# Two Toeplitz layers of a four-layer network: coefficient tables in small pieces, an unpadded product tensor, and a projection in two passes by columns

## The chip, the cores and the metric

The kernel runs on one core of a Trainium2 chip. The metric is the device time of one execution in microseconds, given as the median of the runs. The profile is one more execution, recorded instruction by instruction.

## The reference

The input x has 8 samples of 56 x 56 positions with 192 channels, all in f32. Four layers follow each other, each of the form x + layer(group norm of x). Layers 0 and 1 are alike, and the change lies in them:

```python
p = silu(x @ p_w.T + p_b); q = silu(x @ q_w.T + q_b); v = silu(x @ v_w.T + v_b)   # 192 -> 576
a1 = rpe_mlp(lags, t1...) * decay; a2 = rpe_mlp(lags, t2...) * decay              # 111 lags x 576
qv = q * v
o1 = toeplitz(qv along w, a1); o2 = toeplitz(qv along h, a2)
out = (p * (o1 + o2)) @ o_w.T + o_b                                               # 576 -> 192
```

A Toeplitz product along one axis is, for each of the 576 channels, a 56 x 56 matrix whose entries depend on the lag alone, multiplied by the 56 values of a row or column. Layer 2 is a 7 x 7 depthwise convolution with an MLP, layer 3 a windowed attention.

## The kernel before

Samples are worked on in pairs: `j0 = 0` and `j0 = 2` each stand for two of the four pairs, that is for half of the batch. Each of the two layers has, for each half, three generators that emit instructions and yield their estimated time:

- Q(i, j0), `tno_qv` (L221): for tokens in groups of 256, it loads x (L237, on SP), normalizes it (L243, on ACT), multiplies it by the weights of q and v in units of 128 tokens and 512, 512 and 128 columns (L260, on PE), adds the bias (L269, on DVE), applies silu (L298, ACT), multiplies q by v (L301, POOL) and stores the product in DRAM (L304, SP), in the tensor `qv` of half j0. The loop over columns lies inside the loop over tokens. The first Q is special: its first two groups go through `half_unit` (L281), so that it can begin when the statistics of the first pair are there.
- TZ(i, j0), `tno_toeplitz` (L362): for 9 blocks of 64 channels, and for both axes d (so 18 rounds n), it loads `qv` into the tile `q` (L376 for d = 0, two strided loads; L379 for d = 1, one load of 128 rows, 64 for each half of the block, of which 56 hold data and 8 hold zeros) and the matrices `tm` (L389, four loads), multiplies (L402), copies the result out of the banks (L409, ACT), turns it (L420, L422, DVE), adds the second axis (L424, POOL) and stores the sum (L434, POOL's queue). The loads of round n + 2 are issued when round n has been emitted.
- O(i, j0), `tno_out` (L474): for tiles of 224 tokens, it loads x and the sums (L119, L499), makes p (L527 to L546), multiplies (L553) and projects (L562 to L588), stores the next x and takes its statistics.

A channel block of TZ needs `qv` of all tokens, for its own 64 channels. A pass of Q yields all channels at once.

`decay_tables` (L136) makes the Toeplitz coefficients of one layer: powers of the decay (L146 to L158, DVE), a small MLP (L179 on PE, L181 on DVE), and for each of two axes and five channel groups one matmul (L185), two operations on DVE (L192) into a tile `a` of which there are two, and up to four stores to DRAM (L202). It is a plain function: everything is emitted where it is called.

`tno_layers` (L666) sets the order. First comes a head, in which the statistics of the input (`input_stats`, L207) and the first Q are interleaved by hand, the tables of layer 0 and of layer 1 are called at two places, and rows of zeros are written to `qv` (L715). Then `weave` (L629) runs lanes: the generators of a lane one after the other, and beside them the steps of one TZ. It gives TZ its next step when

```python
want = (done / total - lo) / (hi - lo) * given     # lo 0.04, hi 0.92
while steps is not None and gave < want: ...
```

so that TZ advances in proportion to the lane's estimated time; whatever remains of TZ is emitted when the last generator of the lane has come to 0.9 of its time. From the first TZ on, PE, ACT, DVE and POOL run in the order in which instructions were emitted. The lanes before are:

```python
lanes = [[(first, QT - 104.0)], [(Q(0, 2), QT)], [(O(0, 0), OT), (Q(1, 0), QT)]]
lanes += [[(O(0, 2), OT), (Q(1, 2), QT)], [(O(1, 0), OT)], [(O(1, 2, False), OT)]]
```

with QT = 298.1 and OT = 299.6. Beside lanes 1 to 4 stand TZ(0,0), TZ(0,2), TZ(1,0) and TZ(1,2). Lane 5 runs beside the convolution of layer 2.

Of the kernel before, what the change touches and what calls it, by code (L numbers as in the profile page):

```python
# [12 lines left out]
F32 = mybir.dt.float32  # L13
# [13 lines left out]
B, H, W, C = 8, 56, 56, 192  # L27
T = H * W
# [15 lines left out]
class Net:  # L44
# [91 lines left out]
    def decay_tables(self, L, p, tables):  # L136

        nc, inp = self.nc, self.inp
        tv = p.tile([32, 111], F32, name="tv", bufs=1)
        nc.sync.dma_start(tv, inp["tvec"])  # L140
        pows = []
        for c in range(5):
            m = min(128, D1 - 128 * c)
            sl = p.tile([128, 1], F32, name="sl")
            nc.sync.dma_start(sl[:m], inp[f"{L}_slope"][128 * c : 128 * c + m, :])
            nc.vector.tensor_scalar(sl[:m], sl[:m], 0.0, 1.0, ALU.max, ALU.min)  # L146
            nc.vector.tensor_scalar(sl[:m], sl[:m], 1.0 - 0.95, 0.95, ALU.mult, ALU.add)
            pw = p.tile([128, 64], F32, name="pw", bufs=5)
            nc.gpsimd.memset(pw[:m, 0:1], 1.0)
            n = 1  # L150
            while n < 64:
                nc.vector.tensor_scalar(
                    pw[:m, n : 2 * n], pw[:m, 0:n], sl[:m], None, ALU.mult
                )
                n *= 2
                if n < 64:
                    sq = p.tile([128, 1], F32, name="sl")
                    nc.vector.tensor_mul(sq[:m], sl[:m], sl[:m])  # L158
                    sl = sq
            pows.append(pw)  # L160
        for d in range(2):
            t = f"{L}_t{d + 1}"
            w0 = p.tile([32, 2], F32, name="w0")
            nc.sync.dma_start(w0[:, 0:1], inp[f"{t}_w0"])
            nc.sync.dma_start(w0[:, 1:2], inp[f"{t}_b0"])
            ws = p.tile([32, 3, 32], F32, name="ws")
            nc.sync.dma_start(ws, inp[f"{t}_ws"])
            bs = p.tile([32, 3], F32, name="bs")
            nc.sync.dma_start(bs, inp[f"{t}_bs"])
            wo = p.tile([32, D1], F32, name="wo")  # L170
            nc.sync.dma_start(wo, inp[f"{t}_wo"])
            bo = p.tile([128, 5], F32, name="bo")
            nc.sync.dma_start(bo, inp[f"{t}_bo"])
            h = p.tile([32, 111], F32, name="h")
            nc.vector.tensor_scalar(h, tv, w0[:, 0:1], w0[:, 1:2], ALU.mult, ALU.add)
            nc.vector.tensor_scalar(h, h, 0.0, None, ALU.max)
            for i in range(3):
                hp = self.bank2()[:32, 0, :111]
                nc.tensor.matmul(hp, ws[:, i, :], h, start=True, stop=True)  # L179
                h = p.tile([32, 111], F32, name="h")  # L180
                nc.vector.tensor_scalar(h, hp, bs[:, i : i + 1], 0.0, ALU.add, ALU.max)  # L181
            for c in range(5):
                m = min(128, D1 - 128 * c)
                ap = self.bank2()[:, 0, :111]
                nc.tensor.matmul(  # L185
                    ap[:m], wo[:, 128 * c : 128 * c + m], h, start=True, stop=True
                )
                a = p.tile([128, 4 * self.TG + 56], F32, name="a")
                nc.gpsimd.memset(a[:m, 111:], 0.0)
                back = view(pows[c][:m], 55, [[-1, 55]])  # L190
                for lo, hi, dec in ((0, 55, back), (55, 111, pows[c][:m, 0:56])):
                    nc.vector.scalar_tensor_tensor(  # L192
                        view(a[:m], 110 - lo, [[-1, hi - lo]]),
                        ap[:m, lo:hi],
                        bo[:m, c : c + 1],
                        dec,
                        ALU.add,
                        ALU.mult,
                    )
                for n in range(m // 32):  # L200
                    to = tables[d][self.TG * (4 * c + n) : self.TG * (4 * c + n + 1)]
                    nc.sync.dma_start(  # L202
                        to.rearrange("g (c w) -> c g w", w=self.TW),
                        view(a[32 * n : 32 * n + 32], 0, [[4, self.TG], [1, self.TW]]),
                    )

    def input_stats(self, xs, gn, j, p):  # L207

# [9 lines left out]
        for more in self.all_norms():  # L218
            pass

    def tno_qv(self, L, j0, xs, gn, qv, apart=None):  # L221

# [117 lines left out]
        for g in range(2 if apart else 0, groups):  # L342
            x, t0, n = loaded.pop(0)
            for s in range(0, n, 128):
                m = min(128, n - s)
                for c0 in range(0, 2 * D1, 512):
                    k = min(512, 2 * D1 - c0)

                    if late is not None:
                        multiply(*late)  # L350
                    if c0 == 512 and s + 128 >= n and g + 1 < groups:
                        normalize(*loaded[0])
                    z = p.tile([128, 512, 4], F32, name="t8")
                    unit(x, s, m, c0, k, z)
                    late = (m, k, z, t0 + s, c0)
                    if c0 == 0 and s == 0 and g + 2 < groups:
                        loaded.append(load(g + 2))
                    yield 5.3 * k / 512
        multiply(*late)
# [2 lines left out]
    def tno_toeplitz(self, j0, mats, qv, o):  # L362
# [6 lines left out]
        def load(n):  # L369
            blk, d = divmod(n, 2)  # L370
            q = p.tile([128, H, 128], F32, name="q", bufs=2)
            if d == 0:

                for half in range(2):
                    of = qv[2 * blk + half, :T].rearrange("(h w) e -> w h e", w=W)
                    nc.sync.dma_start(q[64 * half : 64 * half + W], of)  # L376
            else:
                of = qv[2 * blk : 2 * blk + 2].rearrange("n (h w) e -> (n h) (w e)", w=W)
                nc.sync.dma_start(q.rearrange("p i e -> p (i e)"), of)  # L379
            return q  # L380

        def matrices(n):
# [283 lines left out]
    def tno_layers(self, x0, x1, x2, gn, last):  # L666
# [11 lines left out]
        ]  # L678
        qvs = {

            j0: self.dram.tile([D1 // 32, 64 * W, 128], F32, name=f"qv{j0}") for j0 in (0, 2)
        }
        o = [self.dram.tile([B // 2, 9, 128, T], F32, name=f"{L}_sum") for L in LS]
        x = (x0, x1, x2)
        with ExitStack() as ctx, ExitStack() as wqp:
            self.wqp = wqp.enter_context(tc.tile_pool(name="wqp", bufs=1, side="right"))
            self.tp = ctx.enter_context(tc.tile_pool(name="tp", bufs=3))
            Q = lambda i, j0, apart=None: self.tno_qv(LS[i], j0, x[i], gn[i], qvs[j0], apart)
            O = lambda i, j0, woven=True: self.tno_out(LS[i], j0, x[i], gn[i], o[i], x[i + 1], gn[i + 1], woven)
            TZ = lambda i, j0: self.tno_toeplitz(j0, tables[i], qvs[j0], o[i])  # L690
            QT, OT, TZT = 25 * 2.25 * 5.3, 28 * 10.7, 8 + 72 * 3.2
# [1 line left out]
            with tc.tile_pool(name="tab", bufs=2) as tab:  # L693
                stats = [self.input_stats(x0, gn[0], j, tab) for j in range(4)]
                for more in stats[0]:
                    pass
                first = Q(0, 0, tab)
                next(first)

                for n in range(14):  # L700
                    next(first)
                    next(stats[1], None)
                for more in stats[1]:
                    pass
                for n in range(10):
                    next(first)
                self.decay_tables("L0", tab, tables[0])
                for st in stats[2:]:
                    for more in st:
                        next(first)  # L710
                none = tab.tile([112, 512], F32, name="none", bufs=1)
                nc.gpsimd.memset(none, 0.0)
                for qv in qvs.values():
                    to = qv[:, T:].rearrange("n (p k) e -> p n (k e)", p=112)
                    nc.gpsimd.dma_start(to, view(none, 0, [[0, D1 // 32], [1, 512]]))  # L715
                self.decay_tables("L1", tab, tables[1])
                for t in tables:
                    for d in range(2):
                        nc.gpsimd.dma_start(t[d][D1 // 32 * self.TG :, :512], none[:1])
                lanes = [[(first, QT - 104.0)], [(Q(0, 2), QT)], [(O(0, 0), OT), (Q(1, 0), QT)]]  # L720
                lanes += [[(O(0, 2), OT), (Q(1, 2), QT)], [(O(1, 0), OT)], [(O(1, 2, False), OT)]]
                self.weave(lanes[0], None, lanes[1][0][0])
            in_order = tc.manual_schedule(engines=ENGINES)
            with tc.tile_pool(name="tz", bufs=1) as self.tz, in_order:
                self.tms = []
# [1 line left out]
                    self.tms.append(self.tz.tile([128, 32 * self.TW], F32, name=f"tm{i}"))  # L727
                for n, tz in enumerate((TZ(0, 0), TZ(0, 2), TZ(1, 0), TZ(1, 2))):
                    self.weave(lanes[n + 1], tz, lanes[n + 2][0][0], TZT)
                    if n == 2:  # L730
                        wqp.close()
            self.weave(lanes[5], **last())


# [906 lines left out]
```

## Time and profile before

| | us |
|---|---|
| median of three runs (lowest, highest) | 5861.83 (5849.73, 5865.73) |
| the profiled execution | 5859.99 |
| its span | 5858.2 |
| PE busy in it | 5356.5 (91%) |
| DVE, ACT, POOL busy | 2365.6, 2269.0, 2206.4 |
| mean granted clock of PE | 0.954 |

Of the groups of instructions, the costliest is L260 on PE with 1286.6 us; L402 has 525.6 us. In the tables by stretch below, each row is a stretch of the span in us from its start, then its length, and the time in it in which each engine was busy, with the number of instructions in brackets; then come the granted clock of PE (1.00 is full), the mean busy share of the 16 DMA engines (packets overlap, so that it may pass 1) and the rate in GB/s. A line of waits names who waited, for what, how many us in total, how often, and the longest.

### The profile page before, as it was taken

How to read it: one execution, taken by the hardware profiler on the slowest of the kernel's cores; microseconds unless marked ns; L12 is line 12 of the kernel's file. 1: busy time of each engine (PE TensorE's matmuls, PEld its weight loads, DVE VectorE, ACT ScalarE, POOL GpSimd, SP SyncE). 2: the span in 40 equal slices, each digit the busy share in tenths (PEclk: the TensorE clock that was granted, in tenths of full speed). 3: DMA queues.
4: the chain of work that ended last, by engine and by line, in shares of the span. 5: the costliest groups of instructions: out<-in, count | busy, mean ns of one | idle time of the engine just before them, and what ended most of it. 6: DMA issues, size and time to landing. Idle time of an engine off the chain costs nothing.

```text
span 5858.2 us, 144266 instructions
## 1 busy us (share of the span) xinstructions
PE 5356.5 (91%) x64672; PEld 3886.7 (66%) x64672; DVE 2365.6 (40%) x3770; ACT 2269.0 (39%) x2990; POOL 2206.4 (38%) x1527
## 2 busy tenths in 40 slices
PE   5799888899999999999888799989999999889887
PEld 2577666677777777777666578856665445667666
DVE  5444554233454233553343322331222322556655
ACT  2244454444454444554444322242323333333332
POOL 1244566466556564565666300000001001333332
PEclk8799999999999999999999899999999999999998
DMA  8547998898787887987999465644444222344442
GB/s 268 110 144 219 267 287 245 220 264 275 214 237 217 239 258 224 254 249 196 312 296 293 168 210 205 230 125 161 150 160 121 64 64 62 75 97 86 89 92 56
DMA packets 1029770, 1098.79 MB, mean 188 GB/s; under 512 B 232768, under 2 KB 966976, under 8 KB 1013728
## 3 DMA queue, kind: packets, MB, share of 16 engines
q1 hardware_dynamic: 993568, 888.57, 55.5%
q0 software_dynamic: 35584, 200.99, 8.9%
q8 instruction: 509, 8.34, 0.6%
q14 instruction: 109, 0.89, 0.0%
HBM read 725.48 MB, written 363.94 MB: 186 GB/s over the span
## 4 chain that ended last, share of the span: by engine, by line
PE 57%; POOL 6%; SPq 6%; DMA 5%; DVE 5%; issue 3%; ACT 2%; POOLq 0%; DVEq 0%; ACTq 0%
PE bank L260 9%; PE bank L950 6%; PE bank L811 5%; PE bank L527 4%; PE bank L1030 4%; PE bank L572 4%; PE bank L402 4%; SPq L389 3%; PE bank L1044 3%; POOL s L424 2%; PE bank L1224 2%; PE bank L536 2%; PE bank L575 2%; SPq L376 2%; PE bank L1171 2%
## 5 line engine op out<-in xcount | busy, mean ns | idle before, releaser
L260 PE MATMUL bank<-wq,t 128*128 128x256 f32 (+4 forms) x7680 | 1286.6, 375 | 66.8 <-DVE t L269 36.3
L260 PEld LDWEIGHTS bank<-wq,t 128*128 128x128 f32 (+2 forms) x7680 | 1006.5, 191 | 348.1 <-issue 110.5
L269 DVE TENSOR_TENSOR t<-bank,wq 128x1024 f32<-128x1024 f32 (+3 forms) x480 | 517.8, 1111 | 776.6 <-PE bank L260 575.1
L301 POOL TENSOR_TENSOR t<-t 128x1024 f32<-128x1024 f32 (+2 forms) x288 | 518.7, 1815 | 692.4 <-ACT t L298 371.5
L409 ACT COPY ot<-bank 128x896 f32<-128x896 f32 x576 | 493.2, 914 | 626.8 <-PE bank L402 351.3
L424 POOL TENSOR_TENSOR s<-s,ot 128x1568 f32<-128x1568 f32 x144 | 618.3, 4298 | 70.0 <-DVE ot L422 69.3
L402 PE MATMUL bank<-q,tm 56*32 56x224 f32 x18432 | 525.6, 365 | 81.6 <-DMA tm<-L_tab 26.8
L298 ACT ACTIVATE t<-t 128x2048 f32<-128x2048 f32 (+2 forms) x288 | 422.0, 1488 | 405.7 <-DVE t L269 396.1
L402 PEld LDWEIGHTS bank<-q,tm 56*32 56x32 f32 x18432 | 354.4, 109 | 221.6 <-issue 115.8
L553 POOL TENSOR_TENSOR t<-t,t 128x896 f32<-128x896 f32 x168 | 347.3, 2085 | 358.4 <-DMA t<-L_sum 163.9
L527 PE MATMUL bank<-t,wo 128*128 128x224 f32 x1792 | 398.0, 378 | 46.6 <-ACT t L506 22.1
L585 DVE SCALAR_TENSOR_TENSOR t<-bank,wo,t 128x448 f32<-128x448 f32 x112 | 76.4, 682 | 886.3 <-ACT t L581 474.7
L950 PE MATMUL bank<-z,w 128*128 128x448 f32 (+1 forms) x1344 | 413.7, 555 | 1.9 <-ACT h L959 1.7
L527 PEld LDWEIGHTS bank<-t,wo 128*128 128x128 f32 x1792 | 352.4, 203 | 83.8 <-issue 31.7
L546 ACT ACTIVATE t<-bank,wo 128x448 f32<-128x448 f32 x448 | 248.1, 635 | 407.2 <-PE bank L536 379.2
L572 PE MATMUL bank<-t,wo 128*128 128x224 f32 x1792 | 378.1, 365 | 0.0
L127 POOL DMA_DIRECT2D x<-x x64 | 36.6, 573 | 859.7 <-DVE x L981 829.6
L572 PEld LDWEIGHTS bank<-t,wo 128*128 128x128 f32 x1792 | 337.2, 194 | 33.8 <-issue 32.2
L811 PEld LDWEIGHTS bank<-xt,cm 113*112 113x112 f32 x3072 | 315.0, 180 | 43.7 <-issue 38.3
L420 DVE STREAM_TRANSPOSE s<-ot 128x1792 f32<-128x1792 f32 x144 | 292.5, 2033 | 124.3 <-DMA L_sum<-s 102.1
L811 PE MATMUL bank<-xt,cm 113*112 113x108 f32 (+2 forms) x3072 | 326.2, 266 | 6.4 <-issue 3.3
L950 PEld LDWEIGHTS bank<-z,w 128*128 128x128 f32 (+1 forms) x1344 | 182.2, 189 | 205.7 <-issue 197.4
(148 smaller groups left out, 6991.3 us busy)
## 6 DMA issues: line engine op xcount, KB each, us to landing
q<-qv SPq DMA_DIRECT2D x36, 3584.0 KB
q<-qv SPq DMA_DIRECT2D x72, 1568.0 KB
L_sum<-s POOLq DMA_DIRECT2D x288, 392.0 KB, 7.4
t<-L_sum SPq DMA_DIRECT2D x112, 1008.0 KB
qv<-t SPq DMA_DIRECT2D x192, 512.0 KB
cm<-in_L_cm SPq DMA_DIRECT2D x96, 896.0 KB
tm<-L_tab SPq DMA_DIRECT2D x288, 240.0 KB
x<-t POOLq DMA_DIRECT2D x112, 336.0 KB, 7.1
```

Of the source, the lines that this page charges most:

```text
L260: nc.tensor.matmul(pp[:m, b, 256 * j : 256 * j + k], x[rows, j, 2 if part else b, s : s + m], w[rows, part, c0 + c : c0 + c + k],  start=p ...
L269: nc.vector.tensor_add(z[:m, c : c + k, :], view(pp[:m], 0, [[1, k], [256, 4]]), view(bias[:m], c0 + c, [[1, k], [0, 4]]),)
L298: nc.scalar.activation(z[:m, :n, :], z[:m, :n, :], AF.Silu)
L301: nc.gpsimd.tensor_mul(prod[:m, :k], half[:, :, 0], half[:, :, 1])
L402: nc.tensor.matmul(pt[32 * j : 32 * j + 32, r, hf * 224 : (hf + 1) * 224], tm[rows, at : at + 32], q[rows, :, 4 * c : 4 * c + 4], start=Tr ...
L409: nc.scalar.copy(view(ot, 4 * (g % 4), [[16, 2], [32, 112], [1, 4]]), view(pt, 0, [[512, 2], [4, 112], [1, 4]]),)
L424: nc.gpsimd.tensor_add(to, to, view(of, 0, [[1, 28], [32, 56]]))
L527: mm(gs[c // 2][:, b, c % 2 * 256 : c % 2 * 256 + N], pw[:, 0, 128 * c : 128 * c + 128], xn[:, b], start=c % 2 == 0, stop=False,)
L553: gate.tensor_mul(to, to, pg)
L572: mm(P[:, b, :N], ow[:, c, 0:128], g[:, 4 * b + c], start=False, stop=c == 3 and b == 1)
L811: nc.tensor.matmul(pc[:, 128 * e + 4 * m0 : 128 * e + 4 * m1], cm[:113, e, k, :], xt[:, m0 - 1 + k : m1 - 1 + k, c + e, :], start=n == 0 a ...
L950: nc.tensor.matmul(phs[c][:, s, :TT], w0[rows, part, at : at + 128], z[rows, Z[2 if part else s], :], start=part == flip, stop=part != flip,)
```

## The change

- `decay_tables` becomes a generator with 21 yields for a layer. Both layers' tables are one stream `decay` of 42 pieces: 14 are taken beside the statistics of the third and fourth pair, one after each step of the first Q, and the remaining 28 beside the rest of the first Q, by `weave` with lo 0 and hi 0.75.
- `qv` has T = 3136 rows for each channel group instead of 64 x 56 = 3584; the writing of zeros goes, and the load for d = 1 becomes two loads of 56 rows. Rows 56 to 63 and 120 to 127 of the tile `q` are not loaded; no matmul reads them.
- `tno_qv` takes a range of columns. Q(1,2) becomes two generators: columns 0 to 511 (channel blocks 0 to 3) in lane 3, behind O(0,2), and columns 512 to 1151 (blocks 4 to 8) at the head of lane 4, ahead of O(1,0). Each of them loads and normalizes x. TZ(1,2) begins at the start of lane 4 as before, which is now behind the first pass and beside the second.
- The pool of the weights of q and v is closed one lane later.

```diff
+            yield 1.0
...
-    def tno_qv(self, L, j0, xs, gn, qv, apart=None):
+    def tno_qv(self, L, j0, xs, gn, qv, apart=None, cols=(0, 2 * D1)):
...
-                for c0 in range(0, 2 * D1, 512):
-                    k = min(512, 2 * D1 - c0)
+                for c0 in range(*cols, 512):
+                    k = min(512, cols[1] - c0)
...
-                of = qv[2 * blk : 2 * blk + 2].rearrange("n (h w) e -> (n h) (w e)", w=W)
-                nc.sync.dma_start(q.rearrange("p i e -> p (i e)"), of)
+                for half in range(2):
+                    of = qv[2 * blk + half].rearrange("(h w) e -> h (w e)", w=W)
+                    nc.sync.dma_start(q[64 * half : 64 * half + H].rearrange("p i e -> p (i e)"), of)
...
-            j0: self.dram.tile([D1 // 32, 64 * W, 128], F32, name=f"qv{j0}") for j0 in (0, 2)
+            j0: self.dram.tile([D1 // 32, T, 128], F32, name=f"qv{j0}") for j0 in (0, 2)
...
-                self.decay_tables("L0", tab, tables[0])
+                decay = (dt for i in range(2) for dt in self.decay_tables(LS[i], tab, tables[i]))
                 for st in stats[2:]:
                     for more in st:
                         next(first)
-                none = tab.tile([112, 512], F32, name="none", bufs=1)
-                nc.gpsimd.memset(none, 0.0)
-                for qv in qvs.values():
-                    to = qv[:, T:].rearrange("n (p k) e -> p n (k e)", p=112)
-                    nc.gpsimd.dma_start(to, view(none, 0, [[0, D1 // 32], [1, 512]]))
-                self.decay_tables("L1", tab, tables[1])
+                        next(decay)
...
-                lanes += [[(O(0, 2), OT), (Q(1, 2), QT)], [(O(1, 0), OT)], [(O(1, 2, False), OT)]]
-                self.weave(lanes[0], None, lanes[1][0][0])
+                parts = [Q(1, 2, None, cols) for cols in ((0, 512), (512, 2 * D1))]
+                lanes += [[(O(0, 2), OT), (parts[0], QT * 4 / 9)], [(parts[1], QT * 5 / 9), (O(1, 0), OT)]]
+                lanes += [[(O(1, 2, False), OT)]]
+                self.weave(lanes[0], decay, lanes[1][0][0], 28.0, 0.0, 0.75)
```

More of the change, by code (lines that the diff above doesn't have):

```diff
@@ L181, in decay_tables @@
                 nc.vector.tensor_scalar(h, hp, bs[:, i : i + 1], 0.0, ALU.add, ALU.max)
+                yield 1.0
             for c in range(5):
@@ L205, in decay_tables @@
                     )
+                yield 1.0
     def input_stats(self, xs, gn, j, p):
@@ L345, in tno_qv @@
                 m = min(128, n - s)
-                for c0 in range(0, 2 * D1, 512):
-                    k = min(512, 2 * D1 - c0)
+                for c0 in range(*cols, 512):
+                    k = min(512, cols[1] - c0)
                     if late is not None:
                         multiply(*late)
-                    if c0 == 512 and s + 128 >= n and g + 1 < groups:
+                    if c0 == max(cols[0], min(512, cols[1] - 512)) and s + 128 >= n and g + 1 < groups:
                         normalize(*loaded[0])
@@ L355, in tno_qv @@
                     late = (m, k, z, t0 + s, c0)
-                    if c0 == 0 and s == 0 and g + 2 < groups:
+                    if c0 == cols[0] and s == 0 and g + 2 < groups:
                         loaded.append(load(g + 2))
@@ L374, in load @@
                 for half in range(2):
-                    of = qv[2 * blk + half, :T].rearrange("(h w) e -> w h e", w=W)
+                    of = qv[2 * blk + half].rearrange("(h w) e -> w h e", w=W)
                     nc.sync.dma_start(q[64 * half : 64 * half + W], of)
             else:
-                of = qv[2 * blk : 2 * blk + 2].rearrange("n (h w) e -> (n h) (w e)", w=W)
-                nc.sync.dma_start(q.rearrange("p i e -> p (i e)"), of)
+                for half in range(2):
+                    of = qv[2 * blk + half].rearrange("(h w) e -> h (w e)", w=W)
+                    nc.sync.dma_start(q[64 * half : 64 * half + H].rearrange("p i e -> p (i e)"), of)
             return q
@@ L687, in tno_layers @@
             self.tp = ctx.enter_context(tc.tile_pool(name="tp", bufs=3))
-            Q = lambda i, j0, apart=None: self.tno_qv(LS[i], j0, x[i], gn[i], qvs[j0], apart)
+            Q = lambda i, j0, *more: self.tno_qv(LS[i], j0, x[i], gn[i], qvs[j0], *more)
             O = lambda i, j0, woven=True: self.tno_out(LS[i], j0, x[i], gn[i], o[i], x[i + 1], gn[i + 1], woven)
@@ L706, in tno_layers @@
                     next(first)
-                self.decay_tables("L0", tab, tables[0])
+                none = tab.tile([1, 512], F32, name="none", bufs=1)
+                nc.gpsimd.memset(none, 0.0)
+                for t in tables:
+                    for d in range(2):
+                        nc.gpsimd.dma_start(t[d][D1 // 32 * self.TG :, :512], none)
+                decay = (dt for i in range(2) for dt in self.decay_tables(LS[i], tab, tables[i]))
                 for st in stats[2:]:
@@ L710, in tno_layers @@
                         next(first)
-                none = tab.tile([112, 512], F32, name="none", bufs=1)
-                nc.gpsimd.memset(none, 0.0)
-                for qv in qvs.values():
-                    to = qv[:, T:].rearrange("n (p k) e -> p n (k e)", p=112)
-                    nc.gpsimd.dma_start(to, view(none, 0, [[0, D1 // 32], [1, 512]]))
-                self.decay_tables("L1", tab, tables[1])
-                for t in tables:
-                    for d in range(2):
-                        nc.gpsimd.dma_start(t[d][D1 // 32 * self.TG :, :512], none[:1])
+                        next(decay)
                 lanes = [[(first, QT - 104.0)], [(Q(0, 2), QT)], [(O(0, 0), OT), (Q(1, 0), QT)]]
-                lanes += [[(O(0, 2), OT), (Q(1, 2), QT)], [(O(1, 0), OT)], [(O(1, 2, False), OT)]]
-                self.weave(lanes[0], None, lanes[1][0][0])
+                parts = [Q(1, 2, None, cols) for cols in ((0, 512), (512, 2 * D1))]
+                lanes += [[(O(0, 2), OT), (parts[0], QT * 4 / 9)], [(parts[1], QT * 5 / 9), (O(1, 0), OT)]]
+                lanes += [[(O(1, 2, False), OT)]]
+                self.weave(lanes[0], decay, lanes[1][0][0], 28.0, 0.0, 0.75)
             in_order = tc.manual_schedule(engines=ENGINES)
@@ L729, in tno_layers @@
                     self.weave(lanes[n + 1], tz, lanes[n + 2][0][0], TZT)
-                    if n == 2:
-                        wqp.close()
+                wqp.close()
             self.weave(lanes[5], **last())
```

## The prediction, as put on record

> **What bounds the kernel now.** I read first where the time lies by stage: a table of busy time by stretch, cut where the lines of one generator end and those of the next begin (columns: stretch and its length, busy us of PE, PEld, DVE, ACT, POOL with instruction counts, granted clock, DMA share, GB/s).
>
> ```profile
> 0.00:505.00 505.00, 399.09 (x2158) 287.76 (x2159) 234.79 (x446) 163.97 (x173) 148.12 (x123) 0.91 0.61 170
> 505.00:1050.00 545.00, 459.67 (x6486) 346.14 (x6485) 266.65 (x189) 254.58 (x290) 316.64 (x177) 0.91 0.94 266
> ...
> 1880.00:2310.00 430.00, 411.86 (x4705) 313.52 (x4703) 129.30 (x192) 179.91 (x302) 244.45 (x162) 0.97 0.88 250
> 2310.00:2706.00 396.00, 386.65 (x4185) 299.96 (x4186) 203.91 (x162) 203.38 (x226) 238.76 (x133) 0.99 0.76 227
> 2706.00:3250.00 544.00, 467.05 (x6727) 354.77 (x6724) 195.83 (x208) 236.70 (x366) 342.53 (x215) 0.92 0.96 281
> ```
>
> Call 0 to 505 the head, 505 to 1050 stage A (Q(0,2) beside the products TZ(0,0)), 1050 to 1880 stage B, 1880 to 2706 stage C (O(0,2), then Q(1,2), beside TZ(1,0)), 2706 to 3250 stage D (O(1,0) beside TZ(1,2)). C is bound by PE: 798.5 of 826 us busy, 0.967. A and D are not: PE is filled to 0.84 and 0.86, and the DMA share is 0.94 and 0.96. From 3250 on the change touches nothing.
>
> Then the head in pieces of 10 and 40 us.
>
> ```profile
> 10.00:20.00 10.00, 0.00 (x0) 0.00 (x0) 2.31 (x5) 0.00 (x0) 0.00 (x0) 1.00 1.03 413
> 20.00:30.00 10.00, 0.00 (x0) 0.00 (x0) 3.36 (x6) 0.00 (x0) 0.00 (x0) 1.00 1.03 385
> 30.00:40.00 10.00, 0.00 (x0) 0.00 (x0) 1.68 (x3) 0.00 (x0) 0.00 (x0) 1.00 1.03 385
> ```
>
> ```profile
> 120.00:160.00 40.00, 13.57 (x46) 8.43 (x46) 16.68 (x35) 8.45 (x12) 8.92 (x13) 0.57 0.89 173
> 160.00:240.00 80.00, 69.18 (x404) 54.85 (x404) 38.93 (x83) 28.11 (x28) 24.40 (x20) 0.93 0.45 121
> 240.00:280.00 40.00, 21.00 (x79) 14.68 (x80) 12.92 (x59) 5.37 (x5) 3.65 (x9) 0.54 0.60 107
> ```
>
> For 40 us nothing runs but a few statistics on DVE, while the DMA engines are full; and there are two dents, at 120 and 240, where L179 to L202 (the coefficients) run alone. The DMA issues and the waits of 100:310 say what holds each.
>
> ```profile
> qv<-none POOLq DMA_DIRECT2D x2, 4032.0 KB, 39.7
> ```
>
> ```profile
> POOL a L189 <- DMA L_tab<-a: 49.8, 12, 9.7
> DVE a L192 <- DMA L_tab<-a: 28.6, 10, 5.8
> PE bank L185 <- DVE a L192: 24.6, 9, 5.6
> ```
>
> The zeros are 8.26 MB that land beside the first loads of x; in a dent each piece waits until the coefficients of two pieces before it have been stored, and PE has nothing else queued.
>
> In stage D the PE waits name loads.
>
> ```profile
> PE bank L402 <- DMA tm<-L_tab: 24.0, 5, 10.1
> PE bank L527 <- ACT ot L409: 15.5, 5, 4.2
> ```
>
> **What the Trainium skill says.** "DMA: Bandwidth & Descriptors", section "Issuing engines are not separate DMA queues": whatever engine issues, the transfers share the same 16 DMA engines. The trace agrees: with POOL's zeros in flight the total is 385 to 413 GB/s, but the 4.82 MB of the first statistics take until 41.5 us. The same page, "Why a DMA increments its semaphore by 16 and not by 1": a DMA uses the largest number of engines up to 16 that divides the slowest dimension of both sides. A load of 128 rows uses 16, one of 56 rows 14; the trace doesn't tell engines apart. "TensorE: Matmul & The Clock Gate", section "What's actually happening": after a few idle us PE's clock falls to half. The trace agrees: 0.57 and 0.54 in the dents, 1.00 from 280 to 505.
>
> **The change, part by part.** The sum is against the profiled execution, 5859.99 us (span 5858.2); the median of the runs is 5861.83, so I add 2 us at the end.
>
> (1) Zeros gone. By 41.5 us the engines moved 8.26 MB of zeros, 7 x 672 KB = 4.82 MB of x and 0.39 MB of pmat. At 385 GB/s the last two take 13.5 us; with some 3 us of start they are there at 17, and the last statistics at 18.5 instead of 43.1. The chain from there to the first L281 matmul took 9.6 us (43.1 to 52.7). The 3.3 MB of weights and x that it also needs take 8.7 us more of DMA and are there at 26. So L281 starts at 28 to 30 instead of 52.7; I take 22 us, bounds 10 (other loads behind fill the gap) and 25. It is all on the path: PE has had nothing to do. POOL's two issues (2.4 us) hid behind the loads.
>
> (2) Coefficients in pieces. Idle PE in the dents is 40 - 13.57 + 40 - 21.00 = 45.4 us; the busy part at full clock would be 7.7 + 11.3 us instead of 34.6, so 15.6 more. Full gain 61 us. The 42 pieces don't vanish: 32 have a matmul that now stands between matmuls of L260, and for 20 of them its bank comes free only when L192 has written its `a`, which waits for the stores of two pieces before, each 4 issues on SP behind the waiting stores of q*v (L304). In the dents such a piece took about 3.4 us (L185 at 142.3, 145.5, 149.2 and 152.6); with 4 banks and DVE half idle most of that is covered by the L260 work between. I take 1 us each, 20 in all; bounds 0 and 68 (3.4 each). Gain 41, bounds 61 and -7. If that cover fails, DVE is held, and L269 behind it on DVE holds PE.
>
> (3) Loads along w without the rows of zeros. 9 loads of 3584 KB in each TZ become 18 of 1568 KB: 4.1 of some 108 MB, 3.8% of its DMA work (355 us below), 13 us at most where DMA binds (A, and half of C and D). If 56 rows use 14 engines, each still carries 8 rows for a pair as before, and nothing is gained on the busiest. I take 3 us for A and 0 elsewhere; bounds 0 and 13 each for A and D. The 36 issues more on SP (median 0.6 us) hide behind loads that are waited for anyway.
>
> (4) Q(1,2) in two passes. First the work of one generator. PE, from stage C: L260 328.8 (Q), L402 127.5 (T), the rest 342 (O). DMA, share times length: A = Q + T = 512, D = O + T = 522, C = 0.88 x 430 + 0.76 x 396 = 679 = O + Q + T; hence T 355, O 167, Q 157. Of Q's bytes a quarter is loads of x, so 39 loads and 118 stores. The second pass repeats the 39, and 13 groups x 6 L243 x 0.59 = 46 us of ACT, which is 45% busy: nothing on the path, bounded by 39 us if each group's burst of 3 us held the copies L409 behind it.
>
> weave lets TZ advance with the lane. In C the lane shrinks from 597.7 to 432.1 units, so O takes 74% of TZ's steps (80% of its loads, two ahead by the order of SP) instead of 52%; in D the lane grows to 465.2, and the second pass takes 36% of the steps. By phase, PE at the fill of 0.967, DMA at the 0.95 that A and D reached, the larger counts:
> C, O: PE (342 + 0.74 x 128)/0.967 = 452; DMA (167 + 0.8 x 355)/0.95 = 475.
> C, first pass: PE (146 + 33)/0.967 = 185; DMA (39 + 52 + 71)/0.95 = 171.
> D, second pass: PE (183 + 46)/0.967 = 237; DMA (39 + 66 + 131)/0.95 = 248.
> D, O: PE (342 + 82)/0.967 = 438; DMA (167 + 224)/0.95 = 412.
> Sum 475 + 185 + 248 + 438 = 1346. At the start of D the first L402 came 28 us after the last L260, with 17 us of PE idle; now 0.04 x 465 = 19 us of L260 lie in between, so 9 are left: 1355 against 826 + 544 = 1370, a gain of 15. New waits on SP: the first loads of TZ(1,2) wait for the last store of the first pass, with loads of x and stores of the second queued behind (before: the loads of O), and the loads of block 4 wait for the last store of the second, with tm and O's loads behind; the second pass ends at 36% of TZ's steps, these loads stand at about 39%, so this store has just been issued: a few us, bounds 0 and 10, inside the 9. Bounds: all at the PE fill 1312 (gain 58), and the case below (loss 106).
>
> Sum: 22 + 41 + 3 + 15 = 81; 5860 - 81 + 2 = 5781.
>
> **Rivals.**
> Full cover: DMA hides behind PE in C and D (1312, gain 58), coefficients cost nothing, 14 engines don't matter: 23 + 60 + 10 + 58 = 151 at most, of which I'd expect 135: 5727. For it: stage B and C reached 0.967 at DMA shares up to 0.89. Against: shares of 1.00 to 1.05 in D between 2800 and 3200.
> The head gives back: pieces stall L269 through DVE, part 2 falls to 5: 5817. For it: the waits on L_tab above. Against: DVE is half idle from 160 on.
> Slower: the low fill of A and D is not a matter of the amount of DMA but of its order. Heavy strided loads (L376) alternate with light ones, and SP takes its queue in order, so that stores of q*v and loads of tm stand behind them. Then C's O phase and all of D are filled to 0.85 as D is now: (437 + 653)/0.85 + 185 + 9 = 1476, a loss of 106, with 66 gained elsewhere: 5902. It decides at a fill of 0.878, where the loss eats those 66 (1090/0.878 + 194 = 1436 against 1370). For it: L402's waits for tm in D. Against: in A and D PE has 459 and 467 us of work to 512 and 522 of DMA, while in the new phases PE has as much as DMA.
> That an edit does nothing is possible for part 3 alone.
>
> **Chances.** Forecast 0.50; full cover 0.20; the head gives back 0.17; slower 0.13. A measurement of this kernel tells 0.3%, 18 us, from no change. The forecast and full cover are faster; of the third case 0.12 is faster and 0.05 within; of the last 0.01 is within and 0.12 slower: 0.82, 0.06, 0.12. The range leaves out the last case and the edge of full cover: 5722 to 5850.
>
> **What would show it.** First L281 near 30 us, not 52; no stretch of the head with a clock of 0.5 after that; the first L402 near 440 instead of 508. C shorter by some 165 us, D longer by some 150, with PE fill above 0.9 and L260 in its first third. If L402 in D waits for q or tm by more than 60 us, the last case holds; if PE waits for L269 or L192 in the head by more than 40, the third. Stage A shorter by 10 or more would refute the 14 engines.

## The result and the profile after

The changed kernel takes 5954.36 us (median of four runs, 5944.53 to 5957.76), the kernel before, run beside it, 5855.78 us (5849.36 to 5865.73). The ratio is 1.0164, with a 95% interval of 1.0143 to 1.0186: slower, by about 99 us, where 81 us less were forecast. The profiled execution has a span of 5951.2 us.

First the table of busy time by stretch for the kernel after, cut at its own stages (columns as in the prediction: stretch, length, busy us of PE, PEld, DVE, ACT, POOL with instruction counts, granted clock, DMA share, GB/s). The rows are the head, A, B, O(0,2), the two passes of Q(1,2), and O(1,0) as far as TZ(1,2) runs beside it; the last three together are C and D.

```profile
0.00:428.00 428.00, 389.00 (x2140) 280.62 (x2142) 232.61 (x444) 162.55 (x172) 145.49 (x121) 0.96 0.64 179
428.00:1016.00 588.00, 470.51 (x6506) 351.11 (x6503) 269.00 (x191) 256.70 (x290) 316.75 (x178) 0.90 0.96 241
1016.00:1890.00 874.00, 813.71 (x8897) 621.65 (x8896) 334.59 (x355) 384.54 (x527) 485.28 (x296) 0.96 0.83 222
1890.00:2402.00 512.00, 455.10 (x5744) 341.99 (x5744) 166.19 (x210) 208.89 (x337) 287.44 (x186) 0.94 0.99 252
2402.00:2879.00 477.00, 419.73 (x4754) 320.53 (x4755) 216.69 (x169) 252.70 (x317) 245.58 (x134) 0.93 0.87 228
2879.00:3340.00 461.00, 414.07 (x5136) 313.23 (x5136) 148.40 (x185) 195.47 (x318) 295.21 (x192) 0.94 0.91 248
```

Read the second row (it takes in 6 us of the head) against the row of A before: the same matmuls, 43 us more, a DMA share of 0.96 instead of 0.94, and yet only 241 GB/s instead of 266. The DMA engines are busier and move less. To compare whole stages across kernels I cut all of them at the same events: the first product of TZ(0,0), the last matmul of Q(0,2) (end of A), the last of Q(1,0) (end of B), and the last product of TZ(1,2) (end of C and D together).

| us | head | A | B | C and D | rest | span |
|---|---|---|---|---|---|---|
| before | 508 | 542 | 829 | 1344 | 2635 | 5858 |
| after | 434 | 581 | 874 | 1416 | 2646 | 5951 |
| difference | -74 | +39 | +45 | +72 | +11 | +93 |

The head did what was forecast, and more. These are rows of the kernel after, at the places shown of before:

```profile
20.00:30.00 10.00, 6.42 (x25) 5.65 (x26) 2.92 (x10) 3.63 (x7) 0.00 (x0) 1.00 1.07 366
30.00:40.00 10.00, 10.00 (x32) 3.46 (x30) 7.32 (x13) 0.98 (x2) 0.00 (x0) 1.00 1.07 374
...
120.00:160.00 40.00, 39.07 (x228) 31.50 (x230) 16.31 (x27) 17.89 (x18) 14.89 (x10) 0.91 0.44 124
160.00:240.00 80.00, 76.59 (x453) 59.62 (x452) 36.98 (x63) 30.65 (x30) 28.69 (x31) 0.96 0.63 143
240.00:280.00 40.00, 37.31 (x225) 28.72 (x223) 25.70 (x70) 17.12 (x20) 15.07 (x9) 0.96 0.45 133
```

The first L284 matmul (L281 before) starts at 28.6 instead of 52.7, and the two dents, with clocks of 0.57 and 0.54, are gone.

The loss begins behind the head, in all stages in which TZ runs. The DMA queues of stage A, before (505 to 1050) and after (428 to 1016), show it; the columns are packets, MB, and the time that the packets took as a share of 16 engines over the stretch.

```profile
q1 hardware_dynamic: 122305, 114.88, 79.8%
```

```profile
q1 hardware_dynamic: 124328, 112.02, 83.0%
```

79.8% of 545 us is 435 us; 83.0% of 588 is 488. The queue carries 2.9 MB less and its packets take 53 us longer. What changed on it are the loads of `q`; before, the list of issues had 36 of 3584 KB and 72 of 1568 KB, after, all are alike:

```profile
q<-qv SPq DMA_DIRECT2D x144, 1568.0 KB
```

The loads for d = 0 are strided and move in packets of 512 bytes, those for d = 1 in packets of 28672 bytes, one for each row of the tile. Counted from the packets of both traces:

| packets of 28672 bytes, whole run | number | median ns | mean ns | sum, us of 16 engines |
|---|---|---|---|---|
| before | 4608 | 1066 | 1170 | 337 |
| after | 4032 | 2147 | 2012 | 507 |

An eighth fewer packets, each twice as long: 170 us of DMA time more. Before, 16 of them are in flight during a load, and 16 x 28672 bytes in 1066 ns are 430 GB/s; after, 14 are in flight, and at some 2200 ns that is 182 GB/s.

How the slower loads reach PE can be followed in the waits of stage A, before and after (who waited, for what, us in total, times, longest):

```profile
POOL t L301 <- DMA qv<-t: 117.3, 15, 22.4
```

```profile
POOL t L304 <- DMA qv<-t: 192.5, 26, 23.2
```

The stores of q*v share SP's queue and the engines with the loads of `q`. When they land later, POOL's product has no free tile and waits 75 us more. From there to PE the way is argued: silu and the addition L272 would come later, and banks would be freed later, but in stage A the addition's own waits for POOL did not grow (75.5 us before, 65.2 after). What the trace does show is PE's waits: in stage A they are 117 us in all after and 85 before. In the list of groups, L260 and L263 (the same matmuls, before and after) show where PE pays over the whole run: the number after the second bar is its idle time ahead of them.

```profile
L260 PE MATMUL bank<-wq,t 128*128 128x256 f32 (+4 forms) x7680 | 1286.6, 375 | 66.8 <-DVE t L269 36.3
```

```profile
L263 PE MATMUL bank<-wq,t 128*128 128x256 f32 (+4 forms) x7680 | 1318.2, 380 | 122.5 <-DVE t L272 65.8
```

The idle time grows by 56 us and the busy time by 32, for the same matmuls: PE's clock is lower where they run, 0.90 against 0.91 in A, 0.96 against 0.98 in B, and 0.93 in the two passes of Q(1,2) against 0.99 in the single one before. And the chain of work that ended last changed hands; before, then after:

```profile
PE 57%; POOL 6%; SPq 6%; DMA 5%; DVE 5%; issue 3%; ACT 2%; POOLq 0%; DVEq 0%; ACTq 0%
```

```profile
PE 48%; DMA 12%; POOL 8%; SPq 7%; DVE 5%; issue 3%; ACT 2%; POOLq 0%; DVEq 0%; ACTq 0%
```

A page of the Trainium skill that the prediction did not use bears on this: "SBUF — State Buffer", section "Door 1: The DMA port swizzle (why `[64,N]` ≈ `[32,N]`)". It says that a transfer's bandwidth depends on how many of the 16 ports of SBUF its partitions reach, that bit 6 of the partition number chooses between the two halves of the ports, and that partitions 0 to 63 reach 8 of them; it gives 196 GB/s for 64 partitions. A load of 56 rows lies in partitions 0 to 55 or 64 to 119, that is in one half; the load of 128 rows reached both. My theory from here on: **the split by halves cost the loads half their rate, and everything else in the change is a gain** ("ports theory" in the expectations below). The rivals: 14 engines instead of 16 (the count of engines and not the ports); the doubled number of issues on SP; and the column passes, as the "slower" case of the prediction had it.

### The profile page after: what moved, and what is told of

Same layout as the page of the kernel before. It is cut to its first block, busy times and chain, and to the rows that moved or that the text cites. A ratio compares the mean times of both kernels' runs of the same rounds, so it can differ in the third digit from the quotient of the medians.

```text
span 5951.2 us, 144419 instructions
## 1 busy us (share of the span) xinstructions
PE 5396.6 (91%) x64672; PEld 3898.3 (66%) x64672; DVE 2369.6 (40%) x3770; ACT 2306.9 (39%) x3068; POOL 2204.0 (37%) x1525
## 4 chain that ended last, share of the span: by engine, by line
PE 48%; DMA 12%; POOL 8%; SPq 7%; DVE 5%; issue 3%; ACT 2%; POOLq 0%; DVEq 0%; ACTq 0%
PE bank L952 6%; PE bank L813 5%; PE bank L263 5%; DMA qv<-t 4%; PE bank L1032 4%; SPq L393 4%; PE bank L576 3%; PE bank L531 3%; DMA t<-L_sum 3%; POOL s L428 3%; PE bank L1046 3%; PE bank L406 2%; SPq L379 2%; PE bank L1226 2%; DMA x<-t 2%
## 5 line engine op out<-in xcount | busy, mean ns | idle before, releaser
L263 PE MATMUL bank<-wq,t 128*128 128x256 f32 (+4 forms) x7680 | 1318.2, 380 | 122.5 <-DVE t L272 65.8
L263 PEld LDWEIGHTS bank<-wq,t 128*128 128x128 f32 (+2 forms) x7680 | 1023.6, 194 | 413.7 <-issue 113.0
L272 DVE TENSOR_TENSOR t<-bank,wq 128x1024 f32<-128x1024 f32 (+3 forms) x480 | 517.7, 1111 | 848.8 <-PE bank L263 561.3
L406 PE MATMUL bank<-q,tm 56*32 56x224 f32 x18432 | 532.2, 363 | 103.8 <-DVE t L272 29.4
L406 PEld LDWEIGHTS bank<-q,tm 56*32 56x32 f32 x18432 | 346.9, 108 | 252.0 <-issue 111.5
```

The costliest lines, as they stand in the source:

```text
L263: nc.tensor.matmul(pp[:m, b, 256 * j : 256 * j + k], x[rows, j, 2 if part else b, s : s + m], w[rows, part, c0 + c : c0 + c + k],  start=p ...
L272: nc.vector.tensor_add(z[:m, c : c + k, :], view(pp[:m], 0, [[1, k], [256, 4]]), view(bias[:m], c0 + c, [[1, k], [0, 4]]),)
L406: nc.tensor.matmul(pt[32 * j : 32 * j + 32, r, hf * 224 : (hf + 1) * 224], tm[rows, at : at + 32], q[rows, :, 4 * c : 4 * c + 4], start=Tr ...
```

## The experiments

Times are medians; ratios are to the kernel before, run beside each, with 95% intervals. The medians of the kernel before lie between 5850.61 and 5859.19 us, so kernels of different groups (1 to 4, 5 to 8, 9 and 10, 11) are better compared by their ratios.

**1 to 3: the loads for d = 1 alone.** Three kernels differ from the kernel before in this one load; each splits it in two. The padded `qv` and its zeros stay.

```diff
 e1_loads56: rows 0-55 of each half; rows 56-63 of each half are not loaded
-                nc.sync.dma_start(q.rearrange("p i e -> p (i e)"), of)
+                for half in range(2):
+                    of = qv[2 * blk + half, :T].rearrange("(h w) e -> h (w e)", w=W)
+                    nc.sync.dma_start(q[64 * half : 64 * half + H].rearrange("p i e -> p (i e)"), of)
 e2_loads64: all 64 rows of each half
+                    rows = slice(64 * half, 64 * half + 64)
+                    nc.sync.dma_start(q[rows].rearrange("p i e -> p (i e)"), of[rows])
 e3_loads_odd: the even rows, then the odd rows
+                    rows = slice(odd, 128, 2)
+                    nc.sync.dma_start(q[rows].rearrange("p i e -> p (i e)"), of[rows])
```

> The kernel before, with only the load along the second axis split into two loads of 56 rows (the zeros are still written, the product tensor keeps its padded rows, no other edit). Ports theory (a load whose 56 rows all lie in one half of the tile's partitions reaches half of the memory's ports, so its 28672-byte packets take 2000 ns and more instead of 1062): stages A and B each longer by 40 to 45 us, C and D together by 50 to 90, 5990 to 6035 in all. Layout theory (the unpadded product tensor makes its loads slow): 5856, packets at 1062. Queue theory (one DMA more per round is what costs): slower too, but with packets at 1062.

> The same, but two loads of 64 contiguous rows, so 16 engines and no row fewer than before. Ports theory: as slow as with 56 rows or slower by some us (5990 to 6050), packets over 2000 ns. Theory of 14 engines (what costs is that two of the 16 engines get none of these rows): 5856, packets at 1062. Queue theory: as slow as with 56 rows, with packets at 1062. Layout theory: 5856.

> The same, but two loads of 64 rows each that take the even and the odd rows of all 128 partitions, so that each spreads over both halves. Ports theory: 5845 to 5880, packets between 1062 and 1300 ns. Queue theory: as slow as with two loads of 64 contiguous rows. Theory of 14 engines and layout theory: 5856.

| | median us (range) | ratio | packets of 28672: number, median ns | A, B, C and D |
|---|---|---|---|---|
| e1_loads56 | 6035.86 (6028.90 to 6057.97) | 1.0305 (1.0278 to 1.0333) | 4032, 2011 | 579, 875, 1445 |
| e2_loads64 | 6064.66 (6062.05 to 6068.66) | 1.0346 (1.0326 to 1.0367) | 4608, 2168 | 587, 881, 1465 |
| e3_loads_odd | 5878.94 (5862.56 to 5880.34) | 1.0032 (1.0016 to 1.0047) | 4608, 1066 | 535, 839, 1355 |

The load alone costs 180 us (5856.16 to 6035.86). With 64 rows 16 packets are in flight, at 2252 ns (204 GB/s), and the loss is larger still, so the number of engines is not the cause. (The page's 196 GB/s for 64 partitions is near it, and so are the 182 for 56 rows.) e3 has the same rows, the same bytes, the same number of loads and of issues as e2; what differs is which rows, and so which partitions, one load takes. Its packets are back at 1066 ns and its median is 23 us above the kernel before (28 by the upper end of the interval), which is the most that the extra issues and the rest of the split cost. Stage A of e2 (505 to 1084, 7 us short of its end) and of e3 (499 to 1043, 9 us past its end) in the table by stretch:

```profile
505.00:1084.00 579.00, 458.06 (x6414) 342.29 (x6414) 260.18 (x184) 249.67 (x281) 311.61 (x175) 0.89 0.98 246
```

```profile
499.00:1043.00 544.00, 458.92 (x6504) 344.52 (x6502) 266.65 (x190) 254.95 (x288) 321.35 (x181) 0.93 0.93 266
```

The same PE work; 0.98 of the engines' time for 246 GB/s against 0.93 for 266.

So it is shown that a load confined to one half is slow, and that spreading the same rows over both halves mends it. That the ports are the reason is not shown. With the partitions, e3 also changes what a load reads: a load of e2 reads one channel group of `qv`, a load of e3 and the one load of 128 rows read two, and no run separates the two sides. And a packet takes about as long with 14 in flight as with 16 (2194 ns after, 2252 in e2); if the eight ports of the page were shared evenly, 14 would take 14/16 of 2252, an estimate of 1970.

**4: everything but the split.** The kernel after with the padded `qv`, one load of 128 rows, and the zeros written from SP's queue in the middle of the head.

```diff
-                for half in range(2):
-                    of = qv[2 * blk + half].rearrange("(h w) e -> h (w e)", w=W)
-                    nc.sync.dma_start(q[64 * half : 64 * half + H].rearrange("p i e -> p (i e)"), of)
+                of = qv[2 * blk : 2 * blk + 2].rearrange("n (h w) e -> (n h) (w e)", w=W)
+                nc.sync.dma_start(q.rearrange("p i e -> p (i e)"), of)
...
+                for qv in qvs.values():
+                    to = qv[:, T:].rearrange("n (p k) e -> p n (k e)", p=112)
+                    nc.sync.dma_start(to, view(none, 0, [[0, D1 // 32], [1, 512]]))
```

> The changed kernel with the padded product tensor and the one load of 128 rows put back; the zeros are written by SP in the middle of the head, where the DMA engines have room, instead of at its start. The pieces and the two passes by columns stay. Ports theory: stage A back at 545 and B at 830, the head as short as in the changed kernel, C and D together 1350 to 1375: 5770 to 5795. If the two passes are what costs in C and D, C and D stay at 1430 to 1450 and the whole is 5850.

Measured: 5781.38 us (5771.45 to 5785.16), ratio 0.9862 (0.9842 to 0.9881); packets at 1066 ns; the stages 441, 544, 829, 1325 us. Its rows in the table by stretch, to be set against those of after:

```profile
0.00:441.00 441.00, 398.94 (x2176) 287.03 (x2176) 234.82 (x447) 166.06 (x177) 147.09 (x122) 0.96 0.69 195
441.00:985.00 544.00, 455.10 (x6470) 342.14 (x6467) 266.21 (x189) 251.98 (x286) 314.92 (x177) 0.92 0.94 266
985.00:1814.00 829.00, 800.88 (x8899) 615.54 (x8898) 335.33 (x356) 384.68 (x528) 485.32 (x296) 0.98 0.82 239
1814.00:2291.00 477.00, 445.36 (x5743) 336.21 (x5741) 166.04 (x210) 208.61 (x337) 287.79 (x186) 0.97 0.96 274
```

A and B are those of before to 2 us; the whole loss of the changed kernel, and 75 us more, comes back with one load (and the zeros that it needs). Between this kernel and the one after lie 173 us of median: by stage -7 (the zeros) in the head, +37 in A, +45 in B, +91 in C and D, +8 in the rest.

**5 to 8: what the other parts are worth.** e5: the kernel before with the column passes alone. e6: the pieces and the late zeros, without the column passes. e7: the kernel before with its zeros moved alone. e8: the pieces alone, the zeros early as before.

```diff
 e7_zeros_late, against the kernel before; the block stands behind the tables of layer 1
-                    nc.gpsimd.dma_start(to, view(none, 0, [[0, D1 // 32], [1, 512]]))
+                    nc.sync.dma_start(to, view(none, 0, [[0, D1 // 32], [1, 512]]))
 e8_pieces, against the kernel before
-                self.decay_tables("L0", tab, tables[0])
+                decay = (dt for i in range(2) for dt in self.decay_tables(LS[i], tab, tables[i]))
                 for st in stats[2:]:
                     for more in st:
                         next(first)
+                        next(decay)
...
-                self.weave(lanes[0], None, lanes[1][0][0])
+                self.weave(lanes[0], decay, lanes[1][0][0], 28.0, 0.0, 0.75)
 e6_head_only, against e4_one_load_late
-                parts = [Q(1, 2, None, cols) for cols in ((0, 512), (512, 2 * D1))]
-                lanes += [[(O(0, 2), OT), (parts[0], QT * 4 / 9)], [(parts[1], QT * 5 / 9), (O(1, 0), OT)]]
-                lanes += [[(O(1, 2, False), OT)]]
+                lanes += [[(O(0, 2), OT), (Q(1, 2), QT)], [(O(1, 0), OT)], [(O(1, 2, False), OT)]]
 e5_columns, against the kernel before: the inverse of these lines, with the ranges of columns in tno_qv
```

> The kernel before, with only the last projection in two passes by columns. Forecast of record: C and D together 15 us shorter, 5840. Full cover: 58 shorter, 5798. The slower rival (the fill of D follows the order of the transfers): 60 to 106 longer, 5916 to 5962.

> The kernel before, with only the head changed: coefficients in pieces, and the zeros written by SP in the middle of the head. Forecast of record: 22 + 41 = 63 shorter, 5793. If the two parts share a gain (one hides in the other): 5800 to 5815.

> The kernel before, with only the zeros moved from the start of the head to its middle. Forecast of record: first L281 matmul 22 us earlier, at about 30 us, and the whole 22 shorter: 5834. If later statistics hold PE instead: 5840 to 5855.

> The kernel before, with only the coefficients in pieces; the zeros are written at the start as before. Forecast of record: 41 shorter, 5815. Rival (the pieces hold DVE and so L260): 5851. Full cover: 5795.

| | median us (range) | ratio | head | C and D |
|---|---|---|---|---|
| e5_columns | 5846.00 (5821.07 to 5856.94) | 0.9994 (0.9982 to 1.0006) | 504 | 1328 |
| e6_head_only | 5784.98 (5782.98 to 5786.99) | 0.9887 (0.9873 to 0.9902) | 438 | 1344 |
| e7_zeros_late | 5839.53 (5821.24 to 5852.35) | 0.9976 (0.9968 to 0.9984) | 492 | 1343 |
| e8_pieces | 5820.46 (5809.65 to 5823.06) | 0.9942 (0.9923 to 0.9961) | 461 | 1347 |

e5: C and D are 16 us shorter in the trace, but the ratio says 4 us, between 11 gained and 4 lost, which is not to be told from no change. e4 and e6 differ by the passes too: by 4 us in the medians, by 15 us in the ratios, with an uncertainty about as large. The column passes lose nothing; what they gain is small and not settled. In the table by stretch of e5:

```profile
1876.00:2356.00 480.00, 446.06 (x5744) 336.12 (x5743) 165.94 (x211) 209.38 (x338) 288.11 (x186) 0.97 0.96 275
2356.00:2794.00 438.00, 407.25 (x4753) 310.52 (x4754) 217.20 (x167) 251.46 (x316) 246.63 (x134) 0.97 0.90 259
2794.00:3230.00 436.00, 403.43 (x5112) 304.71 (x5112) 147.77 (x185) 192.10 (x313) 287.17 (x187) 0.96 0.87 260
```

C's O (to 2344), both passes, and D's O took 469, 201 + 237 and about 435 us, where the prediction had 475, 185 + 248 and 438. PE's fill is 0.93, not 0.85: the "slower" case of the prediction does not happen.

The head: moving the zeros starts L281 at 29.6 (23 us earlier) but the first product only 16 us earlier. The other 7 us go into the second dent: between two matmuls of L260 it is 44 us long (207.5 to 251.9), against 35 before, and the first is 3 us shorter. The moved zeros are issued at 199.9 and 217.0 and so land in it, and the loads of the slopes that the tables begin with stand beside and behind them. Three waits of e7 in its first 500 us; the first was 24.6 us before, the last 7.9, and the second did not appear:

```profile
PE bank L185 <- DVE a L192: 36.9, 9, 16.2
POOL a L189 <- DVE sl L158: 18.5, 1, 18.5
DVE sl L146 <- DMA sl<-in_L_slope: 17.2, 5, 9.2
```

The pieces alone bring the first product 46 us earlier. Both together: 70 us earlier, where the two alone gave 62, and 66 us off the median, where 12 and 31 came off alone. For the first product the place of the zeros accounts for it: in e6 they are issued at 113.7 and 131.4, and there is no dent for them to lengthen. Why the medians differ by more, 23 us, was not followed.

**9: the two halves from two queues.** The kernel after, with the second load of 56 rows issued from ACT's queue.

```diff
+                    eng = nc.scalar if half else nc.sync
-                    nc.sync.dma_start(q[64 * half : 64 * half + H].rearrange("p i e -> p (i e)"), of)
+                    eng.dma_start(q[64 * half : 64 * half + H].rearrange("p i e -> p (i e)"), of)
```

> The changed kernel, with the second of the two loads of 56 rows issued from ACT's queue instead of SP's, so that each DMA engine has rows of both halves of the tile queued at the same time. Ports theory: the engines alternate between the halves, the 28672-byte packets fall from a median of 2147 ns to 1100 to 1500, stage A falls from 588 to 550 to 560, and the whole is 5790 to 5850. If the rate follows from 56 rows on 14 engines and not from the half of the partitions: packets stay at 2000 to 2150 and the time at 5940 to 5960. ACT has one issue more per two rounds, behind which its copies stand: some us at most.

Measured: 5939.89 us (5937.41 to 5951.15), ratio 1.0153 (1.0133 to 1.0173), no different from the kernel after, and the packets take 2036 ns in the median. The ports theory had forecast 1100 to 1500 ns and 5790 to 5850 us; that did not come. The section "Can I just issue two DMAs to hit both halves?" of the same page of the skill says no, with 6% for two transfers at partitions 0 and 64. The trace agrees. It also shows that the two loads hardly met: of the 2016 packets on SP's queue 461 had one of the other half in flight beside them. Those took 1868 ns in the median, and those of ACT's queue that met one took 1945, the others 2068 and 2162. The number in flight stayed at 14 in all, and the few packets (32) that had seven of each half in flight around them took some 1880 ns, not 1066. So a second queue does not mend the change, and to have packets of both halves in flight is by itself not enough, which the ports theory in its plain form would not lead one to expect.

**10 and 11: the strided loads from two queues.** The loads for d = 0 have always been split by halves, in e4 too. e10 is e4 with the second half issued from ACT's queue. e11 cuts each half's load in two of 28 rows, one from SP and one from ACT, so that both queues work on the same half.

```diff
 e10_strided_two_queues
-                    nc.sync.dma_start(q[64 * half : 64 * half + W], of)
+                    eng = nc.scalar if half else nc.sync
+                    eng.dma_start(q[64 * half : 64 * half + W], of)
 e11_same_half
+                    m = 64 * half + W // 2
+                    nc.sync.dma_start(q[64 * half : m], of[: W // 2])
+                    nc.scalar.dma_start(q[m : 64 * half + W], of[W // 2 :])
```

> The version with one load of 128 rows and late zeros, with the second half of the strided loads of the first axis issued from ACT's queue. These loads too write 56 rows of one half, but in packets of 512 bytes. Ports theory: a port took 28672 bytes in 1062 ns, 27 GB/s, and 14 engines at 512 bytes in 52 to 67 ns bring 13 to 17 GB/s to each of 8 ports, so nothing changes: 5770 to 5795. If these loads are held by the ports as well: stage A falls from 550 to 500 to 530 and the whole to 5680 to 5750.

> As the version with the strided loads on two queues, but each half of the tile is cut in two loads of 28 rows, one from SP's queue and one from ACT's, so that two queues are at work on the same half at the same time. If the gain of the two queues came from reaching both halves at once (ports): it goes, 5770 to 5795, and the 512-byte packets are back at 52 to 67 ns in the loads. If it came from two queues as such (more reads in flight on each engine): it stays, 5720 to 5750, with packets at 33 to 45 ns.

| | median us (range) | ratio | 512-byte packets, us of 16 engines | A, B, C and D |
|---|---|---|---|---|
| e4_one_load_late | 5781.38 | 0.9862 (0.9842 to 0.9881) | 1136 | 544, 829, 1325 |
| e10_strided_two_queues | 5732.74 (5729.08 to 5742.40) | 0.9793 (0.9773 to 0.9813) | 913 | 526, 824, 1303 |
| e11_same_half | 5841.52 (5831.73 to 5902.51) | 0.9990 (0.9968 to 1.0012) | 1071 | 559, 846, 1347 |

The first case of e10's expectation was no change. What came has the numbers of its second, that the ports hold these loads as well (A 500 to 530, 5680 to 5750 in all): e10 is 49 us below e4 by the medians, 40 by the ratios, and beats both kernels, the one before by 2.1%. The queues of stage A of e4 (441 to 985) and of e10 (443 to 990, 21 us past its end):

```profile
q1 hardware_dynamic: 121944, 114.92, 80.1%
```

```profile
q1 hardware_dynamic: 100273, 102.26, 60.8%
q10 hardware_dynamic: 27950, 14.25, 10.5%
```

q10 is ACT's queue; with it e10 has 71.3%. e11 met neither of its two cases (5770 to 5795 and 5720 to 5750): it has two queues too and is 60 us slower than e4 by the medians, 75 by the ratios. So a second queue is not enough. That both halves are in flight at once in e10 would explain its gain, and the time of the 512-byte packets falls by 223 us in e10 and by 65 in e11; but e11 also doubles the number of strided loads, and PE then waits for them (41.7 us for `q` between 440 and 3200, in seven waits, where e4 has one of 6.5). Why e11 falls behind e4 was not separated, so the cause of e10's gain stays open.

## Why the prediction was wrong

**Step (3) failed, and it decided the miss.** It took the split of the d = 1 load for a matter of bytes and of engines: "each still carries 8 rows for a pair as before, and nothing is gained on the busiest. I take 3 us for A and 0 elsewhere; bounds 0 and 13 each for A and D." The count was right, 14 packets in flight; but it assumed that a packet takes as long as before. It took 2147 ns instead of 1066. The term measured +37 in A, +45 in B, +91 in C and D, 173 us in all against e4 (and 180 in e1), where it was booked as a gain of 3. Its bounds stopped at 0 with no reason that excludes a loss, and no rival had one there. The trace of before could not have told it: all its loads in packets of 28672 bytes cover both halves of the tile. That is what should have kept the bound open. Why a load in one half is slower stays open between the ports and what the load reads.

Point by point, the rest:

- (1), the zeros: 22 us at the start of L281 were forecast, 23 to 24 measured. All of it was put on the path; alone (e7) only 12 (the median) to 16 us (the first product) arrive, because there the moved zeros lengthen the second dent.
- (2), the pieces: 41 us forecast, 46 at the first product (e8), 31 in the median. Of the 20 us set aside for the pieces, only 3.3 appear as waits of PE for them between 100 and 310 of after (2.7 at L180, 0.6 behind L194); the full gain of 61 less the 46 leaves 15, and where the rest of it went was not followed.
- (1) and (2) together: 63 forecast, 66 in the median of e6, 74 at the first product of after.
- (4), the column passes: 15 forecast, 16 in the trace of e5, 4 by its ratio (between 11 gained and 4 lost), so the term was too large or the gain is nothing. The phases of O and the two passes together came within 6 us; the first pass took 16 us more than forecast and the second 11 less. C, up to the last matmul of the first pass, shrank from 826 to 681 us (1876 to 2557 in e5), so by 145 and not 165.
- The sum without step (3) was 78 us; e4, which has all but that step, is 75 below the kernel before by the medians. That it comes so near is in part luck: alone, (1), (2) and (4) gave some 12, 31 and 4 of the forecast 22, 41 and 15, and the zeros are still written in it.
- The rivals: full cover did not come about, PE's fill in A stayed at 0.84 even in e4. The head gave nothing back. The slower case landed on the right side for the wrong reason: its mechanism, the order of heavy and light transfers in C and D, is refuted by e5, and the loss was as large in stage B, which it did not name.
- Two of the three signs that were to show a step wrong did not appear: in D L406 waits for no load, and in the head PE waits a few us for L272 and L194. The third, "Stage A shorter by 10 or more would refute the 14 engines", looked for a gain only, and A became longer by 39. PE's waits for `q` at the products, whose loads are issued two rounds ahead, hardly grew in A (5.0 us before, 6.4 after); POOL's wait for the stores that share the queue grew by 75.

## What to carry to other kernels

Before a load is cut or its rows changed, ask which partitions each piece touches: here two loads that each lie in one half of the 128 partitions ran at less than half the rate of one load over both (182 and 204 GB/s against 430), and saving an eighth of the bytes did not pay for it. In a table by stretch, a DMA share that stays while GB/s falls says that the transfers have become slower, not more; the packets' own times then show which. And where a step is bounded at "no gain", look for a reason that excludes a loss before the range stops there.

## What the runs showed of the hardware that was not expected

- Whether a load lies in one half of the tile or spans both decides its rate: packets of 28672 bytes took 1062 to 1066 ns with 16 in flight over both halves, 2252 with 16 in one half, 2194 with 14, and 1540 to 1710 when only 7 to 9 were in flight in one half.
- Even and odd rows in two loads (e3) have packets at the full rate: the split itself costs 28 us at most, by the upper end of e3's interval; the half is what costs.
- Issuing the second of two strided loads from ACT's queue gained 49 us by the medians, 40 by the ratios (e10 against e4); the cause is open. "DMA: Bandwidth & Descriptors", section "Issuing engines are not separate DMA queues", says that this saves issue time only; here the time of the 512-byte packets themselves fell from 1136 to 913 us of 16 engines.
